# The seam between causal attention and a mixture of experts, its order written out by hand

## The chip, the cores and the metric

One core of a Trainium2 chip runs the whole program in one launch. The metric is the device time of one execution in microseconds (us). The core has a matrix engine (TensorE, PE), which reads on-chip SBUF and writes the eight PSUM banks of 2 KB per partition; VectorE (DVE) and ScalarE (ACT), which read and write both; GpSimd (POOL), which works on SBUF and issues indirect transfers; and SyncE (SP), which issues most other transfers. Each engine takes its instructions in their order and waits on semaphores that others raise.

## The reference, cut to what matters

Latents `x` of 64 sequences of 32 rows and 256 columns go through two layers of cross attention, attention and a feed-forward block, each added to `x` after a layer norm. The change touches the last two of the six parts: causal self attention with 16 query heads on 4 key groups, and a feed-forward block of 8 experts of which each row takes one.

```python
# causal attention (biases left out)
scores = jnp.einsum('bhqd,bhkd->bhqk', q, k) * (1.0 / np.sqrt(d))
scores = jnp.where(causal[None, None, :, :], -jnp.inf, scores)
attn = jax.nn.softmax(scores, axis=-1)
x = x + jnp.einsum('bhqk,bhkd->bhqd', attn, v)
# experts: one per row, scaled by its probability
route = jax.nn.sigmoid(x @ router_w)
max_ind = jnp.argmax(route, axis=1)
for e in range(num_experts):
    h = jax.nn.silu(x @ gate_w[e]) * (x @ up_w[e])
    out = out + jnp.where((max_ind == e)[:, None], h @ down_w[e], 0.0)
x = x + out * max_prob
```

(In the experts `x` is layer-normed first.) All is float32.

## The kernel before, in words

The 2048 rows are 16 tiles of 128 rows, four sequences each. Every part goes over these tiles; the last two parts share one block, "wE", from L1784 to the end. There the order on PE, DVE and ACT is the order in which the program is written (`manual_schedule`, L1786); POOL and SP are ordered by the framework, which mostly keeps the program's order too.

**Attention, slots t = 0 to 15.** Slot t of the loop at L2094 issues the scores of tile t+1 (`score`, 64 small matmuls into the four-bank tile `S`, L310; DVE adds the mask and takes the maximum, L261 and L270; POOL subtracts it, L271; `power`, the exponential, is ACT's, L1825), the values of tile t+1 (`values`, bank `v`, L1833; `place_values` copies them into `vde`, a quarter on DVE and three on ACT, L1849 and L1851), the transposes of tile t's weights (`heads_on_partitions`, bank `PT`, L279, L281) and the weighted sum of tile t-1 (`gather`, bank `o`, L1858; DVE divides, L1866 and L1868, and POOL adds to `x`, L1871).

**Routing.** Tiles are routed in groups, `ROUTED`: 0 to 3 together, then in twos. A group passes `route_stats` (DVE statistics, L172; then a chain of small POOL operations, L157 to L1571), `route_norm` (ACT, L1577), `route_turn` (four transposes, L1593, and an ACT copy, L1598), `route` (eight matmuls into `lpf`, L1607; an ACT exponential, L1616; DVE operations to the one-hot `oh` and its running count `cum`, L1617 to L1627), `places` (matmuls `rank`, L1635 and L1638, and DVE operations to each row's slot, L1642 to L1647) and `send`, per tile: a cast of the slots (L1652) and an indirect transfer from POOL, which writes the tile's rows to their places in a DRAM array `srt`, sorted by expert (L1655).

**Tables.** `give_out` (L1671) counts the rows per expert that are routed so far (`cnt`, L1677) and works out, in a chain of small DVE operations, which expert tiles are sure to be full: a table of start rows (`rowi`) and one of weight offsets (`tei`). It is called four times, when 10, 12, 14 and all 16 tiles are routed (`EARLY`); the calls give the expert tiles 0 to 2, 3 and 4, 5 and 6, and 7 to 19 (`FIRST` = 0, 3, 5, 7, 20). A running `done` (L1720) holds what earlier calls gave. `give_halves` (L1729) serves the last four tiles, which mix two experts.

**Expert tiles j = 0 to 19.** `load_rows` (SP reads a table entry, then a transfer of 128 rows from `srt`, L1915, ordered after all sends so far), `rows_norm` (DVE, L1945, and the index cast `ti`, L1949), `rows_turn` (two transposes `tps`, L1961, and the ACT copy `xTs`, L1963), `gate` and `up` (PE reads the weight offset, then 2 x 2 passes of 512 columns each, L2005), `hidden_of` (ACT tanh, L2035; DVE L2036 and L2037), `turn_hidden` (four transposes `tph`, L2044, and a DVE copy `hT`, L2049), `down` (eight passes of 256 columns, L2005; DVE scales and adds, L2060; POOL scatters the rows to the output, L2063). Names such as `loads_to(n)` and `norms_to(n)` bring these steps up to tile n-1.

**The seam.** Before the change, the first expert tile's gate stands in slot 13 of the loop, the second in slot 14; from L2161 a written list interleaves tiles 2 and 3 with slot 15 and the last routing; the loop at L2202 takes tiles 4 to 19, and in its first pass the last routing and the last table. The order around the first gate, in slot 13, is this (L2130 to L2145):

```python
m = t - (NT - 3)
if m == 0:
    norms_to(2)
    rows_turn(0, "mm")
if m >= 0:
    gate(m)
    up(m)
    hidden_of(m)
...
turned[t] = heads_on_partitions(sc.pop(t), ps1, t, work, "e")
```

Of the kernel before, what the change touches and what calls it, by code (L numbers as in the profile page):

```python
# [13 lines left out]
P = 128  # L14
# [6 lines left out]
NE = 8  # L21
# [26 lines left out]
def perceiver_kernel(ctx: ExitStack, tc: tile.TileContext, a: dict, out: bass.AP):  # L48
# [346 lines left out]
    with tc.tile_pool(name="wA", bufs=2) as work, tc.tile_pool(  # L395
# [59 lines left out]
        def power(t):  # L455
            nc.scalar.activation(sc[t], sc[t], AF.Exp)
# [1087 lines left out]
    nc.vector.memset(done, 0.0)  # L1544
    slots = w1.tile([P, NT], mybir.dt.uint32, name="slots")
# [84 lines left out]
    def places(ts, ps, tag):  # L1630

        n_ = len(ts)
        gs = slice(ts[0], ts[0] + n_)
        rank = ps.tile([P, n_ * NE], F32, tag=tag, name=f"rank{ts[0]}")
        nc.tensor.matmul(  # L1635
            rank, tri, oh[:, gs, :].rearrange("p t e -> p (t e)"), start=True, stop=False
        )
        nc.tensor.matmul(  # L1638
            rank, one, cum[:, gs, :].rearrange("p t e -> p (t e)"), start=False, stop=True
        )  # L1640
        sl = sm(f"slr_{ts[0]}", [P, n_, NE])
        nc.vector.tensor_tensor(  # L1642
            sl, rank.rearrange("p (t e) -> p t e", e=NE), bc(base, 1, n_), ALU.add
        )
        nc.vector.tensor_tensor(sl, sl, oh[:, gs, :], ALU.mult)
        slf = sm(f"slf_{ts[0]}", [P, n_])
        nc.vector.tensor_reduce(slf, sl, AX.X, ALU.add)  # L1647
        for i, t in enumerate(ts):
            place[t] = slf[:, i : i + 1]
# [21 lines left out]
    def give_out(n_tok, ps, tag):  # L1671


        last, z = n_tok == NT, EARLY.index(n_tok)
        n = FIRST[z + 1] - FIRST[z]
        cnt = ps.tile([P, NE], F32, tag=tag, name=f"cnt{n_tok}")
        nc.tensor.matmul(cnt, one, cum[:, n_tok, :], start=True, stop=True)  # L1677
        n_t = w1.tile([P, NE, NT], F32, tag="n_t", name=f"n_t{n_tok}")
        nc.vector.tensor_tensor(
            n_t, bc(cnt, 2, NT), bc(n128h if last else n128e, 1, NE), ALU.is_gt  # L1680
        )
        left = w1.tile([P, NE], F32, tag="left", name=f"left{n_tok}")
        nc.vector.tensor_reduce(left, n_t, AX.X, ALU.add)
        if n_tok > EARLY[0]:
            nc.vector.tensor_sub(left, left, done)
        upto = w1.tile([P, NE], F32, tag="upto", name=f"upto{n_tok}")
        nc.vector.tensor_tensor_scan(upto, one[:, 0:NE], left, 0.0, ALU.mult, ALU.add)

        L = NE - 1
        te = w1.tile([P, n, L], F32, tag="te", name=f"te{n_tok}")  # L1690
        nc.vector.tensor_tensor(
            te, bc(ntile[:, 0:n], 2, L), bc(upto[:, 0:L], 1, n), ALU.is_ge
        )
        tef = w1.tile([P, n], F32, tag="tef", name=f"tef{n_tok}")
        nc.vector.tensor_reduce(tef, te, AX.X, ALU.add)
        tei = w1.tile([P, n], I32, name=f"tei{n_tok}")
        nc.vector.tensor_scalar_mul(tef, tef, float(FE))
        nc.vector.tensor_copy(tei, tef)

        step = w1.tile([P, L], F32, tag="step", name=f"step{n_tok}")  # L1700
        nc.vector.tensor_scalar(step, left[:, 0:L], -1.0, float(NT), ALU.mult, ALU.add)
        if n_tok > EARLY[0]:
            nc.vector.tensor_sub(step, step, done[:, 0:L])
            nc.vector.tensor_add(step, step, done[:, 1:NE])
        nc.vector.tensor_tensor(te, te, bc(step, 1, n), ALU.mult)
        row = w1.tile([P, n], F32, tag="row", name=f"row{n_tok}")
        nc.vector.tensor_reduce(row, te, AX.X, ALU.add)
        nc.vector.tensor_add(row, row, ntile[:, 0:n])
        if n_tok > EARLY[0]:
            nc.vector.tensor_scalar(row, row, done[:, 0:1], float(P), ALU.add, ALU.mult)  # L1710
        else:
            nc.vector.tensor_scalar_mul(row, row, float(P))
        rowi = w1.tile([P, n], I32, name=f"rowi{n_tok}")
        nc.vector.tensor_copy(rowi, row)
        if not last:

            nc.vector.tensor_scalar(upto, upto, float(n), 0.0, ALU.subtract, ALU.max)
            nc.vector.tensor_sub(left, left, upto)
            nc.vector.tensor_scalar_max(left, left, 0.0)
            nc.vector.tensor_add(done, done, left)  # L1720
            return rowi, tei
        rows_n = w1.tile([P, NE], F32, name="rows_n")
        nc.vector.tensor_copy(rows_n, cnt)
        kept.update(cnt=rows_n, left=left, upto=upto, row=row, tef=tef)
        return rowi, tei
# [58 lines left out]
    with tc.tile_pool(name="wE", bufs=2) as work, tc.tile_pool(  # L1784
# [32 lines left out]
        def score(t):  # L1817
            g, i = divmod(t, 4)
            qT, kd, xT = feats[g]
            s_ps = ps_s.tile([P, 4, 512], F32, tag="S", name=f"S_e{t}")  # L1820
            scores(s_ps, qT, kd, i)
            sc[t] = softmax_rows(s_ps, t, work, "e")
# [53 lines left out]
        steps_n = {6: R[0], 8: R[1], 10: R[2], 11: R[3], 13: R[4]}  # L1876
        steps_r = {7: R[0], 9: R[1], 11: R[2], 12: R[3], 14: R[4]}
        steps_p = {8: R[0], 10: R[1], 11: R[2], 12: R[3], 14: R[4]}
        sends = {9: (0, 1), 10: (2, 3), 11: (4, 5), 12: (6, 7)}

        def router_parts(t):

            fns = []
            if t in steps_r:
                fns.append(lambda: route(steps_r[t], ps2, "mm"))
            if t in (11, 12, 14):
                fns += 2 * [lambda: None]
            if t in steps_p:
                fns.append(lambda: places(steps_p[t], ps2, "mm"))
            return fns  # L1890
# [6 lines left out]
        def give(n_tok, ps, tag):  # L1897
            table[EARLY.index(n_tok)] = give_out(n_tok, ps, tag)
# [53 lines left out]
        def turn_rows_to(j):  # L1952
            for j_ in range(len(rowsT), min(j, NS)):
                rows_turn(j_)
# [84 lines left out]
        def turn_hidden(j, tag=None):  # L2039
# [9 lines left out]
            nc.vector.tensor_copy(hT, tp)  # L2049
# [27 lines left out]
        def scatter(ts):  # L2077
            places(ts, ps1, next(banks))
            for t in ts:
                send(t)  # L2080
# [13 lines left out]
        for t in range(NT - 1):  # L2094
# [4 lines left out]
            if t == EARLY[0] + 2:  # L2099
                parts.append(lambda: [send(t_) for t_ in R[3]])  # L2100
                parts.append(lambda: give(EARLY[0], ps2, "mm"))
            if t > 0:
                score(t + 1)
# [16 lines left out]
            if t == NT - 2:  # L2120
                turn_hidden(0, "mm")
                rows_turn(2, "PT")
# [7 lines left out]
            m = t - (NT - 3)  # L2130
            if m == 0:
                norms_to(2)
                rows_turn(0, "mm")
            if m >= 0:
                gate(m)
                up(m)
                hidden_of(m)
            if m == 1:
                down(0, "mm")
            turned[t] = heads_on_partitions(sc.pop(t), ps1, t, work, "e")  # L2140
            for fn in parts[3:]:
                fn()
            if m == 0:
                rows_turn(1, "mm")
                norms_to(3)  # L2145
            if t in steps_n:
                route_turn(steps_n[t], work, ps2, ("mm", "o"))
            place_values(t + 1, v_ps.pop(t + 1))
# [7 lines left out]
            if t == EARLY[0] + 2:  # L2156
                loads_to(FIRST[1])
            if t == NT - 2:
                norms_to(FIRST[1])

        gu_banks()  # L2161
        turned[NT - 1] = heads_on_partitions(sc.pop(NT - 1), ps1, NT - 1, work, "e")
        turn_hidden(1, "v")
        for t_ in ROUTED[-3]:
            send(t_)
        gather(NT - 2)
        route_norm(p12)
        gate(2)
        give(EARLY[1], ps1, "v")
        up(2)  # L2170
        hidden_of(2)
        loads_to(FIRST[2])
        down(1, "mm")
        route_stats(NT - 2)
        turn_hidden(2, "v")
        turn_routed(p12, "mm")
        norms_to(FIRST[2])
        gather(NT - 1)
        banks = iter(("PT", "v", "mm", "o") * 99)
        route_stats(NT - 1)  # L2180
        route(p12, ps1, next(banks))
        turn_rows_to(4)
        gate(3)
        up(3)
        scatter(p12)
        hidden_of(3)
        down(2)
        route_norm(p14)
        give(EARLY[2], ps1, next(banks))
        turn_hidden(3)  # L2190
        turn_rows_to(5)
        turn_routed(p14)
        loads_to(FIRST[3])
# [8 lines left out]
        for j in range(4, NS + 1):  # L2202
# [4 lines left out]
            if j == 4:  # L2207
                route(p14, ps1, next(banks))
# [3 lines left out]
            if j == 4:  # L2212
                scatter(p14)
                norms_to(FIRST[3])
# [6 lines left out]
            if j == 4:  # L2221
                give(NT, ps1, next(banks))
# [4 lines left out]
            if j >= 5:  # L2227
                loads_to(j + 6)
                norms_to(j + 4)
# [96 lines left out]
```

## Time and profile before

| what | value |
|---|---|
| median of three runs | 1204.37 us (1201.12 to 1208.15) |
| the profiled execution | 1198.35 us |
| its span, first to last instruction | 1196.4 us |
| mean granted clock of TensorE | 0.974 |
| PE busy over the span | 1127.1 us (94%) |
| DVE, ACT, POOL busy | 782.5, 550.4, 386.4 us |
| gates of tiles 0 to 6 start at | 1033.91, 1046.57, 1057.72, 1071.93, 1081.45, 1093.55, 1100.25 us |
| scores of tiles 14 and 15 start at | 1022.82 and 1041.78 us |

A row of the trace in order of time gives the start, the duration, the engine, the line, the operation, output and inputs, and how many instructions are merged (x8); in brackets stands how long the engine sat idle just before, and whose instruction ended that. The duration of a merged row reaches from its first start to its last end. "PE busy" counts a matmul as long as it runs, so a slow clock makes PE look busier. The granted clock is 1.00 at full speed and 0.50 at half.

### The profile page before, as it was taken

The numbers are of one execution on the slowest core, as the hardware profiler recorded it, in microseconds if no ns is written. First come the engines' busy times: TensorE is split into PE (matmuls) and PEld (weight loads), VectorE is DVE, ScalarE is ACT, GpSimd is POOL, SyncE is SP. The second block draws the span as 40 slices with busy tenths as digits, with TensorE's granted clock in tenths as the row PEclk, the third lists the DMA queues.
The fourth block names the chain that finished last, engine by engine and source line by source line (L and its number), as shares of the span: only waits on it lengthen the run. The fifth ranks groups of instructions, "written<-read, shape, count | busy, mean of one in ns | idle before, by whom it ended". The sixth has DMA issues, their size and how long they took to land. (4 is left out here: it accounts for less than half of the span.)

```text
span 1196.4 us, 25839 instructions
## 1 busy us (share of the span) xinstructions
PE 1127.1 (94%) x10008; PEld 783.9 (66%) x10008; DVE 782.5 (65%) x1860; ACT 550.4 (46%) x1287; POOL 386.4 (32%) x490
## 2 busy tenths in 40 slices
PE   8999999999999998999999999999999888788897
PEld 5556766767676747569667777766766656555553
DVE  5776247778978987654257676777676565656543
ACT  2437354455463572241356666556566455321110
POOL 2443346767675875200000000011020356332111
PEclk9999999999999999999999999999999998779999
DMA  5121122564455455761041121212110463102413
GB/s 147 56 74 38 32 85 85 180 166 122 123 152 159 129 154 171 220 168 58 16 97 31 27 54 28 54 28 54 28 27 1 150 191 113 38 27 63 150 33 117
DMA packets 98987, 109.03 MB, mean 91 GB/s; under 512 B 37240, under 2 KB 73465, under 8 KB 98642
## 3 DMA queue, kind: packets, MB, share of 16 engines
q1 hardware_dynamic: 97138, 103.05, 30.3%
q0 software_dynamic: 1728, 4.33, 1.0%
q8 instruction: 80, 1.31, 0.5%
q14 instruction: 41, 0.34, 0.1%
HBM read 76.36 MB, written 31.41 MB: 90 GB/s over the span
## 5 line engine op out<-in xcount | busy, mean ns | idle before, releaser
L1374 ACT ACTIVATE pp<-Sd,nm 128x257 f32<-128x257 f32 x256 | 118.2, 474 | 63.3 <-DVE nm L1370 62.3
L823 PE MATMUL qb<-xT_b,b_q 128*128 128x256 f32 x512 | 121.3, 385 | 0.0
L823 PEld LDWEIGHTS qb<-xT_b,b_q 128*128 128x128 f32 x512 | 94.7, 190 | 39.1 <-issue 21.0
L914 PE MATMUL yb<-b_o,oTb 128*128 128x256 f32 x512 | 113.6, 380 | 0.5 <-DVE oTb L906 0.5
L914 PEld LDWEIGHTS yb<-b_o,oTb 128*128 128x128 f32 x512 | 96.3, 190 | 14.3 <-issue 1.6
L1370 DVE TENSOR_REDUCE nm<-Sd 128x2 f32<-128x514 f32 x128 | 82.6, 686 | 34.1 <-PE Sd L1362 34.1
L1383 DVE TENSOR_TENSOR pp<-pp,rd 128x514 f32<-128x514 f32 x128 | 88.9, 695 | 2.1
L1399 ACT COPY pTd<-pt 128x512 f32<-128x512 f32 x112 | 61.4, 597 | 40.9 <-PE pt L1393 40.9
L1362 PE MATMUL Sd<-ct,qTd 64*128 64x257 f32 x480 | 68.6, 404 | 1.3 <-ACT pp L1374 1.3
L842 POOL TENSOR_TENSOR q2b<-qTb 128x512 f32<-128x512 f32 x64 | 64.6, 1038 | 15.7 <-ACT qTb L831 15.7
L1414 PE MATMUL od<-pTd,na 128*64 128x256 f32 x480 | 66.7, 397 | 2.8 <-ACT pTd L1399 1.4
L1393 PE MATMUL pt<-cst,pp 128*128 128x128 f32 x512 | 67.3, 275 | 0.0
L831 ACT COPY qTb<-qb 128x512 f32<-128x512 f32 x64 | 37.4, 585 | 64.8 <-PE qb L823 61.9
L1393 PEld LDWEIGHTS pt<-cst,pp 128*128 128x128 f32 x512 | 59.3, 142 | 9.8 <-issue 5.4
L876 DVE RECIPROCAL rqb<-rqb 128x512 f32<-128x512 f32 x16 | 53.5, 3344 | 17.8 <-ACT rqb L871 17.8
L1189 PE MATMUL qd<-xT_d,d_m 128*128 128x256 f32 x256 | 64.3, 395 | 0.2 <-ACT xT_d L246 0.2
L685 PE MATMUL yc<-c,hc 128*128 128x256 f32 x256 | 58.8, 382 | 3.3 <-DVE x L692 3.3
L1433 PE MATMUL yd<-d_n,co 128*128 128x256 f32 x256 | 59.5, 386 | 0.3 <-DVE co L1421 0.3
L1189 PEld LDWEIGHTS qd<-xT_d,d_m 128*128 128x128 f32 x256 | 46.7, 192 | 17.0 <-issue 6.4
L890 DVE RECIPROCAL rdb<-denb 128x512 f32<-128x512 f32 x16 | 53.6, 3353 | 5.7 <-PE denb L888 5.6
L685 PEld LDWEIGHTS yc<-c,hc 128*128 128x128 f32 x256 | 47.7, 190 | 11.7 <-DVE x L692 4.5
L1433 PEld LDWEIGHTS yd<-d_n,co 128*128 128x128 f32 x256 | 47.3, 190 | 12.0 <-issue 5.8
(418 smaller groups left out, 2290.9 us busy)
## 6 DMA issues: line engine op xcount, KB each, us to landing
srt<-pad SPq DMA_DIRECT2D x17, 1040.0 KB
mb<-maskd SPq DMA_DIRECT2D x64, 128.0 KB
ct<-ctd SPq DMA_DIRECT2D x30, 257.0 KB
rct<-in_ctxT_dram SPq DMA_DIRECT2D x32, 128.5 KB
rrt<-in_ctxT_dram SPq DMA_DIRECT2D x64, 64.2 KB
ctd<-rct SPq DMA_DIRECT2D x32, 128.5 KB
nad<-rna SPq DMA_DIRECT2D x16, 256.0 KB
fw<-in_f_wg_dram SPq DMA_DIRECT2D x16, 256.0 KB
```

The lines of the kernel that those rows point to most:

```text
L685: nc.tensor.matmul(y_ps, hs[f][:, i * P : (i + 1) * P], c_2[:, f, :], start=(f == 0), stop=(f == 7),)
L823: nc.tensor.matmul(q_ps[:, hh, :], b_q[:, k, h * P : (h + 1) * P], xT[:, k, c0 : c0 + 256], start=(k == 0), stop=(k == KC - 1),)
L842: nc.gpsimd.tensor_tensor(q2[:, 4 * h4 : 4 * h4 + 4, :], q, q, ALU.mult)
L914: nc.tensor.matmul(y_ps, oT[:, h, :], b_o[:, h, :], start=(h == 0), stop=(h == NH - 1))
L1189: nc.tensor.matmul(q_ps[:, r, :], m[:, k, pr * P : (pr + 1) * P], xT[:, k, c0 : c0 + 256], start=(k == 0), stop=(k == KC - 1),)
L1362: nc.tensor.matmul(s_ps[:, hh, :NKV], qT[hs, b % 8, 4 * u : 4 * u + 4, :], ct[hs, b % 4, :], start=True, stop=True,)
L1370: nc.vector.tensor_reduce(nm, s_ps[:, :, :NKV], AX.X, ALU.max, negate=True)
L1374: nc.scalar.activation(pp[:, hh, :], s_ps[:, hh, :NKV], AF.Exp, bias=nm[:, hh : hh + 1], accum_out=sd[:, hh : hh + 1],)
L1383: nc.vector.tensor_tensor(pp, pp, bc(rd, 2, NKV), ALU.mult)
L1393: nc.tensor.transpose(pt[:, hh * 256 + u * P : hh * 256 + u * P + P], probs[b][:, u, hh, c * P : (c + 1) * P], ident,)
L1414: nc.tensor.matmul(o_ps[64 * hh : 64 * hh + 64, :], na[:, j, c, :], pT[:, c, hh * 256 : (hh + 1) * 256], start=(c == 0), stop=(c == 1),)
L1433: nc.tensor.matmul(y_ps, co[:, pr, :], n[:, pr, :], start=(pr == 0), stop=(pr == 7))
```

## The change

- `give_out` becomes three functions. `give_count` does the count matmul and the operations up to the comparison `te`; `give_rows` makes the two tables of it; `give_done` brings `done` up to date. The arithmetic is the same, but for a vector `jumps` (the differences of `done` plus 16), which `give_done` makes once, so that a later `give_rows` needs one subtraction where three operations stood.
- The attention loop ends after slot 12. Slots 13, 14 and 15 and the expert tiles 0 to 4 are written out as one list; the loop over expert tiles starts at 5.
- The first expert tile moves from slot 13 to slot 14, behind the routing of tiles 10 and 11; the second from slot 14 to slot 15, tile 2 behind it.
- In every slot the places of the next values are copied ahead of the ranks and the routing's transposes. Steps of the written list name other PSUM banks.
- `heat` issues a matmul of constants (the identity with 512 columns of constants) into a bank that the next real matmul overwrites: before the scores in slots 11 to 14 and before the ranks in slots 11 and 12.
- The copy of the turned hidden rows, `hT`, goes from DVE to ACT, for all 20 expert tiles.
- Three more rows' loads are issued in tile 4's step; `norms_to` runs one tile less ahead in the steps of tiles 5 and 6.

```diff
+    def heat(bank, n_):
+        for _ in range(n_):
+            nc.tensor.matmul(bank, ident, cst[:, 0:512], start=True, stop=True)
...
-        rank = ps.tile([P, n_ * NE], F32, tag=tag, name=f"rank{ts[0]}")
+        bank = ps.tile([P, 512], F32, tag=tag, name=f"rank{ts[0]}")
+        heat(bank, idle)
+        rank = bank[:, 0 : n_ * NE]
...
-    def give_out(n_tok, ps, tag):
+    def give_count(n_tok, ps, tag):
...
+        kept.update(z=z, n=n, left=left, upto=upto, te=te)
+
+    def give_rows():
...
+        step = w1.tile([P, L], F32, tag="step", name=f"step{z}")
+        if z:
+            nc.vector.tensor_sub(step, jumps, left[:, 0:L])
+        else:
+            nc.vector.tensor_scalar(step, left[:, 0:L], -1.0, float(NT), ALU.mult, ALU.add)
...
+    def give_done():
...
+        nc.vector.tensor_add(done, done, left)
+        nc.vector.tensor_sub(jumps, done[:, 1:NE], done[:, 0:L])
+        nc.vector.tensor_scalar_add(jumps, jumps, float(NT))
...
             s_ps = ps_s.tile([P, 4, 512], F32, tag="S", name=f"S_e{t}")
+            heat(s_ps[:, 0, :], idle)
             scores(s_ps, qT, kd, i)
...
-            nc.vector.tensor_copy(hT, tp)
+            nc.scalar.copy(hT, tp)
...
-        for t in range(NT - 1):
+        for t in range(NT - 3):
...
             turned[t] = heads_on_partitions(sc.pop(t), ps1, t, work, "e")
+            place_values(t + 1, v_ps.pop(t + 1))
             for fn in parts[3:]:
                 fn()
...
-            place_values(t + 1, v_ps.pop(t + 1))
...
+        t = NT - 3
+        for t_ in R[3]:
+            send(t_)
+        give_count(EARLY[0], ps1, "mm")
+        score(t + 1, idle=1)
+        give_table()
+        loads_to(FIRST[1])
+        route_norm(p10)
+        gather(t - 1)
+        v_ps[t + 1] = values(t + 1)
+        power(t + 1)
+        turn_routed(p10, "mm")
+        turned_of(t)
+        place_values(t + 1, v_ps.pop(t + 1))
+        route_stats(t - 1)
+        give_done()
+
+        t = NT - 2
+        score(t + 1, idle=1)
+        route(p10, ps1, "mm")
+        gather(t - 1)
+        v_ps[t + 1] = values(t + 1)
+        power(t + 1)
+        turned_of(t)
+        norms_to(1)
+        rows_turn(0, "mm")
+        scatter(p10, "o")
+        place_values(t + 1, v_ps.pop(t + 1))
+        gate(0)
+        up(0)
+        route_stats(t - 1)
+        hidden_of(0)
+        norms_to(2)
+
+        t = NT - 1
         gu_banks()
+        turned_of(t)
+        gather(t - 1)
+        turn_hidden(0, "mm")
+        rows_turn(1, "v")
         route_norm(p12)
+        gate(1)
+        give_count(EARLY[1], ps1, "o")
+        turn_routed(p12, "PT")
+        up(1)
+        hidden_of(1)
+        give_table()
+        loads_to(FIRST[2])
+        down(0, "mm")
+        route_stats(t - 1)
+        route(p12, ps1, "v")
+        turn_hidden(1, "PT")
+        norms_to(3)
+        give_done()
+
+        gather(t)
+        rows_turn(2, "mm")
+        scatter(p12, "v")
+        route_stats(t)
         gate(2)
         up(2)
         hidden_of(2)
+        down(1, "PT")
+        route_norm(p14)
+        turn_hidden(2, "mm")
+        norms_to(4)
+        turn_rows_to(4, "v")
+        turn_routed(p14, "o")
+        give_count(EARLY[2], ps1, "PT")
...
         gate(3)
+        route(p14, ps1, next(banks))
         up(3)
         hidden_of(3)
+        give_table()
+        loads_to(FIRST[3])
         down(2)
+        scatter(p14)
         turn_hidden(3)
+        give_done()
+        norms_to(5)
         turn_rows_to(5)
+        gate(4)
+        give_count(NT, ps1, next(banks))
+        up(4)
+        hidden_of(4)
+        down(3)
+        give_table()
+        loads_to(FIRST[3] + 3)
+        turn_hidden(4)
+        norms_to(7)
+        turn_rows_to(6)
...
-        for j in range(4, NS + 1):
+        for j in range(5, NS + 1):
...
+            loads_to(j + 6)
+            norms_to(j + 4 if j > 6 else j + 3)
```

## The prediction

> **What bounds the kernel now.** I read the span in stretches of 20 us first, to find where TensorE (PE) is not full; then stretches of 3.41 us of PE alone, for its clock; then the instructions in order of time from 985 us to the end, for what each idle time waited on. The chain of waits is of no use here: it runs back along the output transfers, which PE does not wait for. Stretches: length, busy us of PE, its weight loads, VectorE (DVE), ScalarE (ACT), GpSimd (POOL), then the granted clock, DMA share, GB/s.
>
> ```profile
> 1000.00:1020.00 20.00, 16.09 (x482) 12.85 (x484) 14.17 (x52) 11.98 (x26) 11.79 (x21) 0.85 0.15 50
> 1020.00:1040.00 20.00, 12.93 (x241) 8.48 (x234) 9.42 (x43) 4.32 (x10) 8.37 (x16) 0.72 0.16 49
> 1040.00:1060.00 20.00, 16.62 (x248) 11.30 (x247) 11.67 (x35) 7.93 (x18) 7.01 (x14) 0.88 0.05 15
> 1060.00:1080.00 20.00, 17.46 (x88) 10.83 (x86) 11.88 (x51) 3.31 (x7) 5.39 (x14) 0.78 0.10 27
> 1080.00:1100.00 20.00, 16.82 (x68) 11.02 (x68) 14.65 (x64) 2.97 (x7) 5.86 (x8) 0.91 0.18 56
> 1140.00:1160.00 20.00, 20.00 (x73) 11.94 (x72) 9.49 (x20) 3.51 (x7) 3.93 (x4) 1.00 0.15 42
> ```
>
> From 1100 us the expert tiles run PE-full at full clock, 5.82 us each (gate of one tile at 1151.38, of the next at 1157.20); nothing of the change shortens that. Only the seam, 1007 to 1106 us, has room: no engine is full there, and the clock is low. Its clock, in stretches of 3.41 us (PE busy, clock, DMA share, GB/s):
>
> ```profile
> 1003.95:1007.36 3.41, 1.93 (x52) 1.00 0.19 66
> 1010.77:1014.19 3.42, 1.49 (x35) 1.00 0.11 39
> 1014.19:1017.60 3.41, 2.92 (x73) 0.50 0.13 41
> 1017.60:1021.01 3.41, 3.41 (x95) 0.50 0.01 2
> 1021.01:1024.43 3.42, 3.15 (x123) 1.00 0.14 44
> 1051.73:1055.15 3.42, 1.80 (x14) 1.00 0.11 38
> ```
>
> The reader is to see a rule of this trace: every change of clock lies on one grid of 3.41 us. After a stretch with 1.80 us busy or less the clock is 0.50; after 1.93 or more it stays. It comes back only after a stretch of at least 3.32 us busy; 2.96 was not enough. Between 1014 and 1093 us ten stretches are at 0.50. The waits of PE behind it:
>
> ```profile
> 1013.64 0.37 PE L1635 MATMUL rank<-oh,tri 128*128 128x16 f32 x2 [1.93 <-DVE oh L1625]
> 1016.79 1.88 PE L1607 MATMUL lpf<-f_r,xTf 128*128 128x8 f32 x8
> 1028.18 1.94 PE L1833 MATMUL ve<-e_v,xT_e 128*32 128x64 f32 x64 [3.67 <-ACT vde L1851]
> 1033.91 5.74 PE L2005 MATMUL gus<-fw,xTs 128*128 x8 [1.42 <-DMA r<-srt]
> 1089.37 0.66 PE L1961 MATMUL tps<-cst,xns 128*128 128x128 f32 x2 [2.27 <-DVE ti L1949]
> 1026.54 0.41 DVE L1849 COPY vde<-ve 32x256 f32<-32x256 f32 x1
> 1065.75 0.68 DVE L2036 SCALAR_TENSOR_TENSOR hs<-hs,gs 128x512 f32<-128x512 f32 x1
> ```
>
> The two DVE rows start where a whole table ends: table 10 runs 1023.13 to 1026.63 (18 operations, 3.50 us), and only then is `ve` copied, ACT copies three more, and PE is let go after 3.67 us. Table 12 (1061.76 to 1065.84) holds the hidden products of tile 2 back the same way. Gate and up take 5.74 us instead of 3.42 as their first five passes last 0.85 each, not 0.43.
>
> **The change, part by part.** Prices: score 0.85, gather 0.68, values 1.10, route 1.06, four transposes 0.60, rank 0.6, count 0.4, gate or up 1.72, down 1.71 on PE; a table 1.05 for the count part, 1.70 for the rows, and 0.83 for `done` on DVE, whose 0.2 us apiece I also take for the two new `jumps` operations; they replace two in each later table (rows there 2.12, now 1.72).
>
> Heat: two passes of 0.43, 0.86, six times: before the scores in slots 11 to 14, before the ranks in 11 and 12. In slot 11 PE ends its transposes at 1011.71 and waits for `oh` until 1013.64. The score product moves that end to 1012.6, the rank product ends at 1013.5, `oh` does not move (it hangs on ACT's norm, done 1011.74, and eight DVE operations): cost nothing. If that cover were gone it is 1.7 us. The stretch that let the clock fall holds then about 3.0 us of work, so slot 12 runs at 1.00: its router takes 1.06, not 1.88, and what this saves (2.7 us) pays its two products (1.7). `oh` of slot 12 still comes at 1020.9, since ACT's exponential ran at 1018.70 and runs about then again. Slot 13 starts at 1022.3, as before. In slots 13 and 14 the score products lie under DVE work (below). Bound of all six: 5.1 us if none is covered, a gain of 3.5 us at best.
>
> By the Trainium skill, "TensorE: Matmul & The Clock Gate", section "Why this matters for your kernels", only idle gaps above about 3 us bring the half clock back. The row speaks otherwise: 1.93 us was enough, in a stretch 1.49 us busy. By the page the slot 11 products would guard against nothing and the sum below would be about 1 us worse.
>
> Slot 13: the places copy now comes ahead of the rank, so `v` is free at once and the 3.67 us stall goes. What is late next is DVE: count 1.05 from 1023.9, mask and maximum of score 14 (1.4, score ends at 1024.8), rows 1.70 to 1028.1, then 0.7, copy 0.4, statistics 0.6, `done` 1.25, to 1031.0. ACT: norm, exponential, three copies, 1.15 for `vde`, to 1032.4, behind POOL, which has the 1.95 us norm chain, then two sends (1.3 each), then the subtraction, to 1029.5. PE is through at 1028.7, score 15 at 1030.5. The sends end at 1028.5; the loads of rows followed them by 2.0 us and landed 2.5 later, so row 0 is there at 1033; before, 1031.0.
>
> Slot 14: router exponential at 1032.6 behind ACT's copies, eight DVE operations (1.92) to 1034.6, 0.7, rows normed at 1035.7. PE waits from 1034.2 for them (1.5 us, nothing falls). Gate 0 at 1036.9, three us later than now, but at full clock: up ends at 1040.3, now 1039.65, and score 15, values 15 and the routing of 10 and 11 are already done. Hidden 0 ready at 1041.2, rows 1 at 1041.8.
>
> Slot 15: gate 1 at 1043.3 (before 1046.57), count, transposes, up, down 0 to 1049.4, router 1050.4. DVE: count to 1046.7, hidden 1 to 1048.5, rows 1050.4, output 0, statistics 1051.5, router 1053.4, rows of tile 2 at 1054. PE waits 2.2 us there; gate 2 at 1054.9 (before 1057.72). Behind it on DVE stand `done`, gather 15, ranks, statistics 15 (1057.4); POOL has two sends first, so the norm chain ends at 1061.3 and ACT's norm at 1062.4, in front of the copies of hidden 2 and rows 3. Gate 3 at 1063.6 (before 1071.93), where half clock on gate 2 would add only 0.3.
>
> Tile 4 is where it is given back. Count, the router of 14 and 15 (1068.5), hidden 3, rows, output 2, ranks, `done` stand ahead of its norm on DVE: 1074.7. PE is done at 1070.8. A wait of 4.8 us: gate 4 at 1075.8 (before 1081.45), and the clock falls for one to two stretches, 1.9 to 3.6 us. Then table 16 (1.45 and 2.05) and output 3 ahead of rows 5: gate 5 at 1087.8 (before 1093.55), 6.0 us to gate 6: 1093.8, before 1100.25. That is 6.4 us.
>
> Hidden copies to ACT: 0.69 off DVE, 0.59 onto ACT, which is 3.5 of 20 us busy: nothing in the steady tiles. Where the half table (4.5 us) holds DVE in tile 6, PE waited 1.71 us for hidden 7; of this 0.65 goes. If ACT were late, at most 0.6 a tile for tiles 0 to 3, where it has norms ahead of it (counted above). Loading three rows earlier, and one norm later in tiles 5 and 6, moves SP and DVE work that waited for nothing there: bounds 0.5 either way, I take 0. Other banks: a transpose of slot 11 waits 0.5 us longer for `slr`, counted; else 0, and 1 us at most, from the 0.49 us wait of such a kind.
>
> Sum: 6.4 + 0.65 = 7 us. The profiled execution took 1198.35 us with a span of 1196.4; it becomes 1191.3. The median of the three runs, 1204.37, is 6 us longer than the profiled one; off it, 1197.4.
>
> **The rivals.** First, no change: a second fall of the clock. The waits before gate 5 (2.5 us for its rows, 0.8 for their copy) can empty a stretch too; two stretches cost 2.7 us, and a register load ahead of a gate (0.5 to 1 us, as between 1032.90 and 1033.88) is not hidden when rows come last, at gates 4 and 5. Seven becomes 3 us: 1201.4. That heat misses its waits, as its bank is not free, belongs here. For it: my waits are in-order queues on DVE with nothing to overtake. Against: before had the same waits and lost more.
>
> Second, slower: the clock is not held after slot 14, where no heat is put. Each stretch at 0.50 costs up to 1.7 us when PE is what ends last. I count two; from four more on the gain is gone, and with eight more, ten in all as now, it is 7 - 13.7 = -6.7: 1211. The trace has ten, but most of them beside waits that I remove, so they cost less there. For it: the waits before gates 2, 4 and 5 all exceed 2 us, and a return needs 3.3 us without a gap.
>
> **How the numbers follow.** The forecast, 1197.4, gets 0.5, with its own range 1190 to 1199; no change 0.33; slower 0.17. At the low end all ten cold stretches vanish and tile 4 waits half as long (7 + 2.7 + 2.4 = 12), and the median may sit 2 or 3 us off (the three runs are 7 us apart): 1189. At the high end stand the whole case of no change, with 3 us of such scatter, and the nearer half of the slower one: 1208. Half a per cent, 6 us, is about what can be told from no change: faster 0.5, same 0.33, slower 0.17.
>
> **What would show it.** Right: the clock at 1.00 from 1014 to about 1070; no wait of `ve` on `vde` above 1 us; heat inside the wait for `oh`; gate 0 later than its neighbours' scores but at 0.43 a pass; gate 3 some 8 us earlier than now; the longest PE wait at the rows of tile 4, ended by DVE. Wrong: stretches at 0.50 in slots 11 to 15, gates 2 to 5 at 0.85 a pass, or rows that land after their norm's turn.

## The result, and the profile after

The changed kernel takes 1208.4 us in the median of 12 runs (1203.21 to 1215.0), the kernel before beside it 1202.36 us (1198.06 to 1208.15): a ratio of 1.0056 [1.0031, 1.0081], 6.7 us (3.7 to 9.7) more. The forecast was 1197.4 us, 7 us less. The profiled execution took 1208.64 us (span 1206.9, mean granted clock 0.975).

The spans of the two profiled executions differ by 10.5 us. I cut them at two marks: the start of slot 11's scores (with the constant product ahead of them, if there is one), and the first transpose of the hidden of tile 6 ("hidden 6" for short); what lies between I call **the seam**.

| stretch | before | after | difference |
|---|---|---|---|
| up to the first score of the attention block | 928.8 | 932.4 | 3.6 |
| slots up to the start of slot 11 | 78.6 | 83.4 | 4.8 |
| the seam | 98.3 | 99.0 | 0.7 |
| from the hidden of tile 6 to that of tile 19 | 81.6 | 83.1 | 1.5 |

Nothing of the change lies in the first row: in the twelve experiments below that mark stands between 932.1 and 939.4 us, as the clock falls at different places of the early parts. The last row is 80.5 to 82.4 us in them, so 1.5 us there is mostly chance too. The second row is not, and the third is where 6.4 us were to be won.

These are the same stretches of 20 us as shown of before (length, busy us of PE, its weight loads, DVE, ACT, POOL, granted clock, DMA share, GB/s), of the changed kernel:

```profile
1000.00:1020.00 20.00, 17.09 (x411) 11.07 (x415) 9.13 (x35) 10.19 (x21) 11.31 (x23) 1.00 0.29 89
1020.00:1040.00 20.00, 16.67 (x475) 11.74 (x467) 15.09 (x60) 8.61 (x20) 13.84 (x23) 1.00 0.12 42
1040.00:1060.00 20.00, 13.87 (x206) 8.86 (x205) 9.76 (x38) 6.61 (x16) 6.85 (x14) 0.91 0.12 36
1060.00:1080.00 20.00, 17.23 (x103) 11.13 (x101) 13.02 (x55) 5.34 (x11) 7.21 (x14) 0.91 0.13 41
1080.00:1100.00 20.00, 13.45 (x50) 8.05 (x49) 12.11 (x56) 2.81 (x6) 4.35 (x6) 0.91 0.12 40
```

The clock is now 1.00 from 1000 to 1040 us, where it was 0.85 and 0.72: that part came true. Behind it PE is emptier than before (13.87 and 13.45 us in the third and the fifth stretch, where it had 16.62 and 16.82). Stretches of 3.41 us (PE busy, clock, DMA share, GB/s) show what empties it; they begin 0.09 us behind the grid on which the clock changes, hence 0.99 and 0.51:

```profile
1041.82:1045.24 3.42, 1.69 (x84) 1.00 0.31 80
1045.24:1048.65 3.41, 0.82 (x7) 0.99 0.01 2
1048.65:1052.06 3.41, 3.41 (x5) 0.51 0.25 83
...
1086.19:1089.61 3.42, 0.73 (x3) 0.99 0.47 153
1089.61:1093.02 3.41, 3.41 (x7) 0.51 0.12 42
...
1099.85:1103.26 3.41, 2.89 (x5) 0.50 0.31 80
```

Five stretches of the seam are at half clock where before had ten (work at half clock is called cold here, at full clock warm): one at gate 0, one at gate 2 (1069.13), one at gate 4 and two at gate 5. Each of the four falls comes behind a stretch in which PE had 0.73 to 1.31 us of work. The waits in front of them, and the rows that answer to those of before (the trace in order of time; in brackets the idle time just before, and what ended it):

```profile
1000.31 1.98 PE L1308 MATMUL qe<-xT_e,e_q 128*128 128x512 f32 x4 [1.29 <-ACT xTf L1599]
1025.78 1.06 PE L1608 MATMUL lpf<-f_r,xTf 128*128 128x8 f32 x8
1027.27 1.08 PE L1850 MATMUL ve<-e_v,xT_e 128*32 128x64 f32 x64
1048.59 5.35 PE L2022 MATMUL gus<-fw,xTs 128*128 x8 [1.54 <-DVE lnb_f L172]
1088.37 0.41 PE L1978 MATMUL tps<-cst,xns 128*128 128x128 f32 x2 [3.57 <-DVE ti L1966]
1089.29 3.60 PE L2022 MATMUL gs<-fw,xTs 128*128 x4 [0.52 <-ACT xTs L1980]
1099.53 0.46 PE L1978 MATMUL tps<-cst,xns 128*128 128x128 f32 x2 [2.45 <-DVE ti L1966]
1100.50 3.78 PE L2022 MATMUL gs<-fw,xTs 128*128 x4 [0.52 <-ACT xTs L1980]
1120.44 0.41 PE L1978 MATMUL tps<-cst,xns 128*128 128x128 f32 x2 [1.59 <-DVE ti L1966]
```

The router of slot 12 (`lpf`) takes 1.06 us, before 1.88; the wait of 3.67 us of `ve` on `vde` is gone. The first row is new: there is no such wait in before. Gate and up of tile 0 (`gus`) take 5.35 us, gates 4 and 5 (`gs`) 3.60 and 3.78 us, where a gate at full clock takes 1.98. Taking off 8.36 us, by which slot 11 starts later (before 1007.43, after 1015.79), the gates start at these times:

| gate | before | forecast | after, less 8.36 | after against the forecast |
|---|---|---|---|---|
| 0 | 1033.91 | 1036.9 | 1040.2 | +3.3 |
| 1 | 1046.57 | 1043.3 | 1049.3 | +6.0 |
| 2 | 1057.72 | 1054.9 | 1060.25 | +5.35 |
| 3 | 1071.93 | 1063.6 | 1069.3 | +5.7 |
| 4 | 1081.45 | 1075.8 | 1080.9 | +5.1 |
| 5 | 1093.55 | 1087.8 | 1092.1 | +4.3 |
| 6 | 1100.25 | 1093.8 | 1101.1 | +7.3 |

The steps go wrong at two places of the seam: up to the end of gate 0 and at gate 5. Gate 0 starts 3.3 us late, gate and up take 1.95 us too long, and so they end 5.3 us late; from there to gate 5 the lag stays within 1 us of that.

### The profile page after: what moved, and what is told of

Read it like the earlier page. It is cut to its first block, busy times and chain, and to the rows that moved or that the text cites. A ratio compares the mean times of both kernels' runs of the same rounds, so it can differ in the third digit from the quotient of the medians.

```text
span 1206.9 us, 25875 instructions
## 1 busy us (share of the span) xinstructions
PE 1133.4 (94%) x10020; PEld 784.9 (65%) x10020; DVE 768.3 (64%) x1840; ACT 561.1 (46%) x1307; POOL 386.7 (32%) x490
## 3 DMA queue, kind: packets, MB, share of 16 engines
q8 instruction: 80, 1.31, 0.5%
## 5 line engine op out<-in xcount | busy, mean ns | idle before, releaser
L685 PE MATMUL yc<-c,hc 128*128 128x256 f32 x256 | 63.1, 402 | 3.3 <-DVE x L692 3.3
L685 PEld LDWEIGHTS yc<-c,hc 128*128 128x128 f32 x256 | 50.6, 201 | 12.9 <-DVE x L692 4.5
```

The costliest lines, as they stand in the source:

```text
L685: nc.tensor.matmul(y_ps, hs[f][:, i * P : (i + 1) * P], c_2[:, f, :], start=(f == 0), stop=(f == 7),)
```

## The experiments

My theory, from these readings, had three causes. **A**: the places copy, moved ahead in every slot, delays ACT's routing copy, and PE with it, in the slots up to 10 too. **B**: the norms of the expert rows stand too late in DVE's order, behind tables and hidden products. **C**: the waits of B empty stretches, so that gates run at half clock. Rivals: the constant products cost what they hold; the first reading of the expert weights makes gate 0 late; the clock matters little, since DVE ends last in any case.

**1. The places copy put back for slots 0 to 10**

```diff
-            place_values(t + 1, v_ps.pop(t + 1))
+            if t > 10:
+                place_values(t + 1, v_ps.pop(t + 1))
...
+            if t <= 10:
+                place_values(t + 1, v_ps.pop(t + 1))
             load_piece()
```

> The changed kernel with one part undone: up to slot 10 the copy of the next values' places stands behind the routing's transposes again, as before. Theory (the place copy ahead of the router's copy on ACT costs slots 6 to 9 some 4.7 us: by the two traces the starts of the scores fall apart by 0.93, 1.41 and 2.39 us in slots 6, 8 and 9): ratio to before 1.0056 - 0.0039 = about 1.0015, and no wait of the query features on the router's copy in slot 9. Rival (those microseconds are chance, the loss lies in the seam): the ratio stays near 1.0056.

0.9991 [0.9965, 1.0017]. Slot 9 lasts 7.99 us, in the changed kernel 10.38, and the wait of query features on `xTf` is gone. The seam stays 99.1 us. These are PE's waits from 925 to 1012 us in the changed kernel (line, releaser: us in total, times, longest), which the kernels with the copy behind do not have:

```profile
PE qe L1308 <- ACT xTf L1599: 1.3, 1, 1.3
...
PE lpf L1608 <- ACT xTf L1599: 0.9, 1, 0.9
```

ACT's three copies into `vde` (1.15 us) go ahead of its copy `xTf`, and the next slot's query features need the bank that this copy empties.

**2. The kernel before, with the copy moved ahead for slots 0 to 10 alone**

```diff
             turned[t] = heads_on_partitions(sc.pop(t), ps1, t, work, "e")
+            if t <= 10:
+                place_values(t + 1, v_ps.pop(t + 1))
...
-            place_values(t + 1, v_ps.pop(t + 1))
+            if t > 10:
+                place_values(t + 1, v_ps.pop(t + 1))
```

> The kernel before with that part alone: up to slot 10 the place copy ahead of the routing's transposes. Theory: 3 to 5 us slower than before, ratio 1.003 to 1.004, with a wait of about 1.3 us of the query features on the router's copy in slot 9. Rival (chance): ratio 1.000 within its interval, no such wait.

1.001 [0.998, 1.004]: not decided by the time. In the trace both waits of A are there, 1.3 and 0.9 us, and slot 9 takes 10.21 us. Over all traces the slots up to slot 11 took 81.9 to 84.2 us in the three kernels with the copy ahead (the changed one, this one, the next), and 76.0 to 81.2, in the mean 79.1, in the eleven with it behind: a difference of the means of 4.0 us. A is shown; 2.2 us of it are the two waits. The rest lies in slots whose length varies with the clock, and how much of it the copy causes is not shown.

**3. No constant products** (nothing else is left out)

```diff
-        for _ in range(n_):
+        for _ in range(0):
             nc.tensor.matmul(bank, ident, cst[:, 0:512], start=True, stop=True)
```

> The changed kernel without its six products of constants. Theory as in the prediction (they lie in waits and hold the clock in slot 12): 1 to 3 us slower than the changed kernel, ratio to before 1.006 to 1.008, the clock at 0.50 in slot 12. Rival (they stand on the path, 0.86 us each): 3 to 5 us faster than the changed kernel, ratio 1.001 to 1.003.

1.0022 [0.9992, 1.0052], the seam 99.1 us. By the time alone this lies where the rival put it (1.001 to 1.003), but the interval reaches into that of the changed kernel (1.0031 to 1.0081), and the seam is as long as with the products. The router of slot 11 is cold (1.88 us; before it was that of slot 12), ten stretches of the seam are at half clock and not five, and slots 11 to 13 last 24.4 us, with the products 22.8; at the hidden of tile 5 nothing is left of that. The products hold the clock, but what they take and what they save come out even in the seam; that they cost something beyond it is not shown, and 6 speaks against it.

**4. Norms of rows earlier in DVE's order** (on top of 1)

```diff
         score(t + 1, idle=1)
+        norms_to(1)
         route(p10, ps1, "mm")
...
         route_stats(t - 1)
+        norms_to(3)
         route(p12, ps1, "v")
...
         hidden_of(3)
+        norms_to(5)
         give_table()
...
         hidden_of(4)
+        norms_to(6)
         down(3)
```

The calls at the old places (one each for rows 0, 2 and 4) go.

> As the first, and besides in the written list the norms of rows 0, 2, 4 and 5 go ahead of the router's and the tables' operations on DVE. Theory (gates 0, 2, 4 and 5 are late since these norms queue on DVE, and the half clock follows those waits): waits of PE for rows 2, 4 and 5 (2.0, 3.6 and 2.5 us) go, gates 4 and 5 at 0.43 a pass; 6 to 9 us faster than the first, ratio about 0.995. Rival (something else is late next, the hidden products or the router's norm): under 2 us faster than the first.

0.9928 [0.9895, 0.996], which is 0.63 per cent or 7.6 us (2.6 to 12.6) under 1. In the trace the seam takes 88.0 us, 11.1 less than in 1, though slot 11's two products ran at half clock in this execution (1.84 us, in the changed kernel 1.02). (What was expected of experiment 9 starts from 87.2 us; that leaves out one of these two products.) The gates stand against the changed kernel, each from the start of slot 11, by -0.1 (gate 0), -0.3 (3), -3.9 (4), -8.0 (5), -11.0 us (6). Gates 4 and 5 of this kernel:

```profile
1087.23 0.38 PE L1978 MATMUL tps<-cst,xns 128*128 128x128 f32 x2
1088.34 1.98 PE L2022 MATMUL gs<-fw,xTs 128*128 x4 [0.73 <-ACT xTs L1980]
...
1095.38 1.98 PE L2022 MATMUL gs<-fw,xTs 128*128 x4 [0.73 <-ACT xTs L1980]
```

The waits of 3.57 and 2.45 us are gone, and with them two cold gates: rows 4 and 5 alone bring some 10.7 us, the clock included. That is B, the largest cause.

**5. Constant products in the bank of the turned rows, the waits left as they are** (on top of 1)

```diff
-            tp = ps1.tile([P, KC, P], F32, tag=tag or next(banks), name=f"tps{j}")
+            bank = ps1.tile([P, 512], F32, tag=tag or next(banks), name=f"tps{j}")
+            heat(bank, {0: 2, 2: 2, 4: 4, 5: 3}.get(j, 0))
+            tp = bank[:, 0 : KC * P].rearrange("p (k q) -> p k q", k=KC)
```

> The first experiment's kernel with further products of constants ahead of the transposes of rows 0, 2, 4 and 5 (2, 2, 4 and 3 of them, 0.86 us each), where PE waits for rows; the waits themselves stay. Theory (the half clock at gates 0, 4 and 5, where passes last 0.85, is worth some 5 us beside the waits): those gates at 0.43 a pass, 3 to 6 us faster than the first experiment, ratio about 0.995. Rival (the passes run slow under waits for DVE anyway): under 1.5 us faster, ratio 0.998 to 1.000.

0.9949 [0.9922, 0.9975], which is 0.42 per cent or 5.1 us (0.6 to 9.5) under 1; the seam 93.6 us, 5.6 less. The rows of tiles 4 and 5 are still late, but their gates run at 0.43 us a pass (1.98 us for four):

```profile
1083.24 1.98 PE L2024 MATMUL gs<-fw,xTs 128*128 x4 [0.52 <-ACT xTs L1982]
...
1092.64 1.98 PE L2024 MATMUL gs<-fw,xTs 128*128 x4 [0.52 <-ACT xTs L1982]
```

The same gates in 1:

```profile
1090.59 3.32 PE L2022 MATMUL gs<-fw,xTs 128*128 x4 [0.52 <-ACT xTs L1980]
...
1101.74 3.46 PE L2022 MATMUL gs<-fw,xTs 128*128 x4 [0.52 <-ACT xTs L1980]
```

From gate 4 to gate 6 it takes 15.3 us, in 1 it was 18.5: 3.2 us. Gate 0 was cold still, but gate and up took 5.37 us, in 1 6.47. Gate 2 is warm too (1.98 us, in 1 3.76), but that brings gate 3 only 0.55 us closer to it: PE then waits 1.01 us for ACT's norm of tiles 14 and 15. So the clock by itself is worth about 5 us here (C); the rival that DVE hides it falls for gates 4 and 5, while at gate 2 most of what was won went into the next wait.

**6. The fourth without constant products**

```diff
-        for _ in range(n_):
+        for _ in range(0):
```

> The fourth experiment's kernel (norms early) without its six products of constants. By the traces of the changed kernel and of the third experiment (99.0 us each from the start of slot 11 to the turned hidden of tile 6) they cost and bring nothing: within 2 us of the fourth, ratio 0.991 to 0.995. Prediction's theory (they hold the clock in slot 12): 2 us or more slower than the fourth. Rival (on the path): 3 us or more faster.

0.9936 [0.9906, 0.9966], the seam 88.8 us, in 4 88.0. As in 3: under 1 us of the seam, nothing in the time.

**7. A product of slot 13 takes its columns from all 48 pieces of the weights** (on top of 4)

```diff
-    def heat(bank, n_):
+    def heat(bank, n_, cols=None):
+        cols = cst[:, 0:512] if cols is None else cols
...
-            nc.tensor.matmul(bank, ident, cst[:, 0:512], start=True, stop=True)
+            nc.tensor.matmul(bank, ident, cols, start=True, stop=True)
...
-            heat(s_ps[:, 0, :], idle)
+            every = fw.rearrange("p (c z) -> p z c", z=NE * 6)[:, 0, :]
+            heat(s_ps[:, 0, :], idle, every if t == NT - 2 else None)
```

> The fourth experiment's kernel; the product ahead of slot 13's scores takes its columns from all 48 pieces of the expert weights instead of the constants. Gate 0 starts 1.6 us after the last rank product in the fourth, though its operand is ready. Theory (its first reading of the weights brings the waits on all their loads into PE's queue, and they take that time): gate 0 starts about 1 us sooner behind the ranks, and slot 13 is as much longer ahead of its scores, under DVE work. Rival (the gap is the reading of the weight offset or of code): the gap stays 1.6 us.

0.9896 [0.9851, 0.9941], of four runs; the seam 88.8 us. Gate 0 came 0.65 us behind the ranks instead of 1.61. From the scores of slot 12 to those of slot 13, with that product between them, it took 8.10 us instead of 7.09, and to those of slot 14 6.48 instead of 7.46. The product itself took 1.93 us instead of 1.02, and behind it the clock was at half for one stretch (from 1028.85), which it was not in 4; so these intervals are not at one clock. I took the shorter gap for support of the first reading; 10 and 12 take it back.

**8. Gate 0 ahead of the ranks and the places copy** (on top of 4)

```diff
+        gate(0)
+        up(0)
         scatter(p10, "o")
         place_values(t + 1, v_ps.pop(t + 1))
-        gate(0)
-        up(0)
```

> The fourth experiment's kernel with gate and up of tile 0 ahead of the ranks and sends of tiles 10 and 11 and of the place copy of slot 14. Theory (gate 0 now waits only for the order: its operand is ready at 1048.1, the ranks wait until 1049.2 for DVE): gate 0 2 to 3 us sooner, the whole 1 to 3 us faster than the fourth, ratio about 0.991. Rival (the sends and the hidden product come later by the same amount, and DVE ends last): as the fourth or slower.

0.9916 [0.9886, 0.9947], the seam 89.1 us. Gate and up took 3.67 us, warm, but PE then waited 3.40 us for the hidden of tile 0:

```profile
1052.49 1.11 PE L2061 MATMUL tph<-cst,hs 128*128 128x128 f32 x4 [3.40 <-DVE hs L2054]
```

Nothing gained over 4: here DVE does end last.

**9. Four and five together** (rows 0 and 2 get products)

```diff
+            heat(bank, {0: 4, 2: 2}.get(j, 0))
```

> The early norms of the fourth experiment, and constant products ahead of the transposes of rows 0 (four) and rows 2 (two), as in the fifth. My theory holds that the two causes add up where they are apart: the early norms already keep the clock at gates 4 and 5, so the products can bring only gate 0 (5.21 us there, 3.5 to 3.7 at full clock) and gate 2 (3.19, then 1.98). If PE is what ends last there, the seam from the start of slot 11 to the turned hidden of tile 6 falls from 87.2 by 2.0 to 2.8 us, to about 84.8, and the ratio is about 0.990. The rival: VectorE and ScalarE set the hidden of tile 0 whatever the clock, as when the gate was moved ahead; then gate 0 is short, a wait of PE behind it grows by the same 1.6 us, and the ratio stays at 0.993.

0.9915 [0.9888, 0.9942]; the seam 88.6 us. Gates 0 and 2 are warm (3.67 us for gate and up, 1.98), and still nothing is gained over 4: from the hidden of tile 2 to that of tile 3 it takes 12.06 us, in 4 it was 8.89. PE is now early and meets the norm of tiles 14 and 15, which hangs on POOL:

```profile
1068.12 1.05 POOL L1662 DMA_INDIRECT srt<-x,slots  x1 [1.20 <-DVE lnf L173]
...
1069.48 0.96 POOL L1662 DMA_INDIRECT srt<-x,slots  x1 [0.30 <-issue]
...
1070.51 0.23 POOL L157 TENSOR_SCALAR lnr_f<-lnf 128x2 f32<-128x2 f32 x1
...
1072.43 1.09 ACT L1578 ACTIVATE xn_f<-x,lnq_f 128x256 f32<-128x256 f32 x2 [4.71 <-POOL lnq_f L1570]
...
1074.37 3.46 PE L2024 MATMUL gs<-fw,xTs 128*128 x4
```

Two sends stand ahead of the chain; ACT's norm stands ahead of its copies of rows 3; gate 3 starts 2.9 us behind the turned rows (1071.47), and cold.

**10. The ninth with the reading of the seventh** (its lines as there)

```diff
+            heat(s_ps[:, 0, :], idle, every if t == NT - 2 else None)
```

> The same, and the product of slot 13 reads one column of each of the 48 pieces of the weights, as in the seventh experiment. My theory: the gap ahead of gate 0 falls from about 1.6 to 0.65 us, slot 13 is 1 us longer, so that against the kernel beside it nothing remains: ratio within 0.002 of that one, about 0.990. The rival: the reading itself was what made the seventh kernel the fastest (0.9896); then this one is 0.003 or more below the kernel beside it.

0.9926 [0.9899, 0.9953], no better than the ninth beside it; the seam 89.7 us. The gap before gate 0 was 1.07 us, and gate 1 was cold (3.26 us).

**11. The kernel before, with the copy of the turned hidden on ACT**

```diff
-            nc.vector.tensor_copy(hT, tp)
+            nc.scalar.copy(hT, tp)
```

> The kernel before, with the copy of the turned hidden on ScalarE instead of VectorE, for all tiles; nothing else. The prediction gave this part 0.65 us, at the half table in the step of tile 6. My theory, after the reading of the changed kernel, is that it gives 0.1 us there (the interval between two turned hiddens 7.70, then 7.60) and nothing elsewhere, so 0.9999. The rival: ScalarE has norms and copies of rows ahead of the copy in the seam's tiles 0 to 4, 0.6 us later each: 1.0015 to 1.0025, seen as waits of the down products on hT above those of the kernel before.

0.9987 [0.9962, 1.0011]: too small for the time. In the trace the interval from hidden 6 to hidden 7 falls from 7.70 to 6.98 us, and the wait for hidden 7 from 1.71 (first row, of the kernel before) to 0.99 (second row, of this one):

```profile
1113.43 0.66 PE L2044 MATMUL tph<-cst,hs 128*128 128x128 f32 x4 [1.71 <-DVE hs L2037]
...
1119.72 0.66 PE L2044 MATMUL tph<-cst,hs 128*128 128x128 f32 x4 [0.99 <-DVE hs L2037]
```

The prediction's 0.65 us is there, and my expectation of 0.1 was wrong. Of the rival, later copies in tiles 0 to 4, the trace shows nothing clear: from gate 0 to gate 6 it takes 65.7 us, before 66.3.

**12. The ninth, with the statistics of tile 15 ahead of the sends of 12 and 13**

```diff
-        scatter(p12, "v")
         route_stats(t)
+        scatter(p12, "v")
```

> The ninth kernel (early norms, constant products ahead of rows 0 and 2), with one exchange in the step of tile 2: the statistics of tile 15, and with them the chain of small GpSimd operations for the norm of tiles 14 and 15, stand ahead of the ranks and sends of tiles 12 and 13. In the ninth kernel the clock at gates 0 and 2 was held, but the turned hiddens of tiles 2 and 3 lay 12.06 us apart (8.89 with cold gates): GpSimd's two sends, 1.05 and 0.96 us from 1068.12, stand ahead of the chain, ScalarE's norm of 14 and 15 starts at 1072.43 behind it, and PE is ready at 1071.88. My theory: GpSimd's queue is what comes last there; without the sends ahead of it the norm starts about 2 us earlier, gate 3 starts about 0.8 us behind the turned rows 3 instead of 2.9, its clock is held, and the interval falls from 12.06 to 9 us or less, so about 3 us in all, ratio 0.989. The rival: the sends, 2 us later, hold the rows of tiles 5 and 6 or the output of tile 1, and what is gained before gate 3 is lost at gates 4 to 6: ratio 0.9915 as before, with waits for rows at gate 5 or 6.

0.9883 [0.9864, 0.9901], the lowest ratio of all, though by the times alone it is not told from 9 (0.32 per cent or 3.9 us under it, -0.1 to 7.8). The interval from hidden 2 to hidden 3 is 8.80 us, 3.26 less. The same chain:

```profile
1067.85 0.27 POOL L157 TENSOR_SCALAR lnr_f<-lnf 128x2 f32<-128x2 f32 x1 [0.77 <-DVE slr L1649]
...
1069.81 1.09 ACT L1578 ACTIVATE xn_f<-x,lnq_f 128x256 f32<-128x256 f32 x2 [1.84 <-POOL lnq_f L1570]
...
1070.58 1.10 POOL L1662 DMA_INDIRECT srt<-x,slots  x1 [0.43 <-issue]
...
1072.84 1.98 PE L2024 MATMUL gs<-fw,xTs 128*128 x4
```

ACT's norm starts 2.6 us earlier (the hidden of tile 2 is turned at 1070.56, in 9 at 1070.31), gate 3 stands 0.9 us behind the turned rows (1071.91) and is warm; gates 4 and 5 wait 0.73 us as in 4, so the later sends held nothing up. The seam is 86.9 us, 1.8 less than in 9 and not 3.3, mainly because gate 1 was cold in this execution (3.68 us, in 9 1.98).

## Why the prediction was wrong, step by step

- **"In every slot" was priced in slot 13 alone.** The places copy ahead was weighed where it removes 3.67 us, and that came true. In the slots up to 10 the same edit puts 1.15 us of ACT ahead of the routing copy; the prediction has no term for it, that is, it put it at nothing without a reason. It cost 4.0 us by the means of the traces (experiments 1 and 2), and nothing was won there. (In slot 14, other than the list of changes says, the ranks still stand ahead of the copy.)
- **Slots 13 and 14, "gate 0 at 1036.9 ... at full clock".** It came 3.3 us later and took 5.35 us for gate and up instead of 3.4: 5.3 us, which all later gates carry. "PE waits 1.5 us, nothing falls" is what failed: PE waited 2.78 us for row 0, then 1.54 us more, and the clock fell. These are rows of the changed kernel (8.36 us to be taken off for the forecast's times):

```profile
1033.38 0.32 PE L310 MATMUL S_e<-kde,qTe 32*32 32x64 f32 x5 [0.44 <-issue]
...
1036.39 0.23 POOL L1570 TENSOR_SCALAR lnq_f<-lnr_f 128x2 f32<-128x2 f32 x1
...
1041.42 0.17 DVE L1741 TENSOR_SCALAR jumps<-jumps 128x7 f32<-128x7 f32 x1
...
1046.29 0.41 PE L1978 MATMUL tps<-cst,xns 128*128 128x128 f32 x2 [2.78 <-DVE ti L1966]
```

DVE was through with `done` and `jumps` at 1041.59, 2.2 us after the forecast (1031.0); the mask and maximum of score 15, the router's operations, the one-hot and the division follow in its order, so that row 0 was normed 2.1 us late. What made DVE late is read from the trace and was not tested: three issue pauses of PE of 0.44 us in slot 13 (1033.38, 1034.13, 1036.07; they stand in 1, 4, 5, 8, 9 and 12 too, not in 7 and 10, and no run says what they are), and small operations that waited for POOL (last section). POOL also put a send in the middle of its norm chain, so that the chain ended only at 1036.6. The other 1.2 us of the 3.3 lie in the gap before gate 0, which stays open.
- **Tile 4 "where it is given back".** The place and the size were right (4.8 us forecast, 3.57 and 0.52 measured). What was not drawn from it is that the order of DVE was the larger lever: 4 moves the norms of four rows and takes 11.1 us out of the seam, the clock that came with it included.
- **Gate 5, in the first rival.** "A second fall of the clock" at 2.7 us came true: two cold stretches, and the lag against the forecast grows from 4.3 to 7.3 us.
- **"Hidden copies to ACT ... 0.65".** Right by itself (11: 0.72). In the changed kernel the interval is 7.60 us against 7.70: the half table now stands ahead of the norm of a row, which the change brings one tile less ahead, and PE waits 1.59 us for that (the row at 1120.44). By this reading the edit "one norm later in tiles 5 and 6", costed at 0, took back what the other gave; no run has it alone.
- **Heat, "cost nothing".** Right for the whole, as far as can be measured (3, 6), and the clock was held up to gate 0. But the five cold stretches that it saved brought nothing in the seam, the products' own time taken off (3), while those at gates 4 and 5 were worth 3.2 us (5).
- **The second rival**, a clock not held after slot 14, was right in kind, but its price of up to 1.7 us a stretch was too high: 5 took five of six cold stretches out of the seam for 5.6 us, 1.1 each. That half clock on gate 2 would add only 0.3 us to gate 3 was nearly right: 5 shows 0.55.

The sum: 4.0 us for the copy, where nothing was forecast, 0.7 for the seam, where -6.4 was, and about 0 at the half table, where -0.65 was, make 4.7 us; measured were 6.7 (3.7 to 9.7). What the rest is stays open; the fall from the changed kernel to 1, 0.65 per cent or 7.8 us (0.3 to 1.0 per cent, the two intervals added in squares), is also larger than the 4.0 us that the traces show. Open as well is the gap before gate 0: it was 1.67 us in 9 and 0.66 in 12, which do the same up to there, so neither the reading of the weights nor the order accounts for it. Two readings of the prediction were wrong by themselves: table 10 has 17 operations, not 18, and the clock's rule was taken from the seam alone (last section).

## What to carry to other kernels

An edit made "in every slot" has to be priced in the slots where the stall it cures does not exist. In a program ordered by hand, look first for the small operation that PE waits for and that stands behind long chains on DVE or POOL; moving it was worth 11.1 us of the seam here (7.6 us by the times), the clock that came with it included, and keeping the clock alone 5.6 (5.1). And a clock that is won may only show the next queue: in 9 it was POOL's two sends, and the interval they held fell by 3.26 us when 12 put the norm chain ahead of them.

## What the runs showed of the hardware

Some small operations of DVE last until an operation of POOL ends that runs beside them. In the changed kernel (DVE's usual time for this is 0.16 us):

```profile
1036.94 1.05 POOL L271 TENSOR_TENSOR s_e<-s_e,mx_e 128x512 f32<-128x512 f32 x1
1036.98 1.03 DVE L1722 TENSOR_TENSOR row<-row,ntile 128x3 f32<-128x3 f32 x1
```

The same stands at 1043.53 (0.64 us, usually 0.17) and, in 9, at 1066.22 (0.73 us, beside POOL's addition of 0.72). All three have two inputs; the reduction at 1043.32, with one, took its usual 0.17 us beside the same operation of POOL. One with a single input did wait in the kernel before (1018.92, 0.65 us). The Trainium skill, "SBUF — State Buffer", has a rule for it: by its section "Who interferes with whom" an operation of VectorE with two SBUF inputs contends with one of GpSimd that reads SBUF, because the second input comes through an interface that both use, and by its section "Summary: rules for kernel authors" the second of the two to issue "fully blocks" until the first is through. The three rows agree. The prediction's walk has no term for it; it is 0.5 to 0.9 us a time in slots 13 and 14.

The clock: all changes of the changed kernel lie on a grid of 3.41 us again. But the bound that the prediction read from before, a fall after 1.80 us busy or less, is no fixed number. Cut on the grid itself, the stretch of the changed kernel from 1041.73 held 1.78 us, that from 956.40 held 1.63, and that of the kernel before from 952.75, in slots that the prediction did not look at, 1.54 us; all three let the clock stand. In 12 it fell after a stretch of 2.24 us (from 1029.14), in 7 after one of 2.72 (from 1025.43). The return is as before: the stretch from 1099.85, 2.89 us busy, did not bring it back, and those of 3.41 did.
